# Two graph-attention layers on one core: every engine's order written by a list scheduler inside the kernel, fixed buffers, and two products moved

## The chip, the cores and the metric

The kernel runs as one program on 1 core of one Trainium2 chip. The metric is the device time of one execution in microseconds (us). The core's engines each run their own instruction stream in the order in which it was written: PE multiplies matrices, DVE and ACT do elementwise work, POOL does little here, and SP issues the transfers. An instruction waits on semaphores for what other engines must have done, and everything behind it on its engine waits too.

## The reference, cut to what matters

32 graphs with 512 nodes and 512 features each; `adj` is a 0/1 matrix with ones on its diagonal. A graph attention layer with 4 heads of 256 features is followed by one with a single head of 512.

```python
def gat_layer(x, mask, W, a_src, a_dst, bias, concat):
    xl = (x @ W).reshape(B, N, H, F)                                   # projection
    asrc = jnp.einsum('bnhf,hf->bnh', xl, a_src)
    adst = jnp.einsum('bnhf,hf->bnh', xl, a_dst)
    e = leaky_relu(asrc[:, :, None, :] + adst[:, None, :, :], 0.2)     # N x N per head
    e = jnp.where(mask[..., None], e, -1e9)
    attn = softmax(e, axis=1)
    out = jnp.einsum('bsdh,bshf->bdhf', attn, xl)                      # product
    return (out.reshape(B, N, H * F) if concat else out.mean(axis=2)) + bias

h = jnp.maximum(_layernorm(x), 0.0)
h = elu(gat_layer(h, mask, W1, att_src1, att_dst1, b1, concat=True))
h = gat_layer(h, mask, W2, att_src2, att_dst2, b2, concat=False)
return x + h
```

## The kernel before, in words

All of it is f32 on PE. For each graph PE does five things:

- four transposes of the normalized input (tiles `pht`, into `ht`);
- the first projection (tiles `pxl_*`, into `xl`): 28 groups of matmuls by a scheme of seven products of blocks instead of eight, whose block sums `hs` DVE forms (lines L336 to L339) and whose partial results ACT copies (L360, L362) or DVE adds (L365) from a PSUM bank into `xl`. A name such as `pxl_0b` is unit 0, bank b; a bank that was copied is written again by a later group, which must wait for the copy;
- the first product (`po`, L420): 4 heads, two groups of 4 matmuls each, weights of attention `p` times `xl`;
- the second projection (`pxm_*`, 14 groups, same scheme), into `xl2`;
- the second product (`po`, L484): 4 groups.

Only graph 0's first projection is done without the scheme (L388), while the weights' columns of scores are still being formed on DVE (L135); the sums of the weights (L109 to L112) come after it.

The softmax of one head (class `Soft`) is a chain over engines. `rows` sends the source scores through a small DRAM buffer and back, spread over all partitions (`das`, `oas`). `first` makes for each of four tiles a Prelu on ACT (L285), a masked minimum on DVE (L288, one custom instruction with the turned mask `mt`) and an Exp with a sum on ACT (L292); then Ln (L295), three small DVE operations and a transpose on DVE. `turn` sends that through DRAM again (`drr<-orr`, then `orr<-drr`, L249 and L255). `second` forms the weights `p`: per pair of tiles two DVE operations (L314), one DVE addition of the mask over both (L319), then two Exps on ACT (L321). The masks are turned by transposing transfers, four for a graph (L225), on SP's queue.

The order on PE is written out by hand in the loop over graphs: the first product of graph i+1, then the first projection of graph i+2, the second product of graph i, the second projection of graph i+1, and so on. What DVE, ACT and SP do comes from the framework's own scheduler, by the place in the program and a few priorities (`URGENT`); buffers rotate in pools. At the start PE does graph 0's first projection, graph 1's transposes, graph 0's first product and then graph 1's first projection. At the end stand graph 31's second projection, graph 30's second product, graph 31's second product.

Of the kernel before, what the change touches and what calls it, by code (L numbers as in the profile page):

```python
# [1 line left out]

# [19 lines left out]
URGENT = 300  # L22


def rows_of(ap, n):

    return bass.AP(tensor=ap.tensor, offset=ap.offset, ap=[[0, n], [1, ap.shape[-1]]])


@with_exitstack  # L30
def tile_gat(
# [30 lines left out]

    nc = tc.nc
# [8 lines left out]
    W = FH + 2  # L72
    assert N == 512 and D == 512 and DO == D and FH == 256 and H == 4

    const = ctx.enter_context(tc.tile_pool(name="const", bufs=1))
    work = ctx.enter_context(tc.tile_pool(name="work", bufs=2))
    psum = ctx.enter_context(tc.tile_pool(name="psum", bufs=1, space=PSUM))
    dram = ctx.enter_context(tc.tile_pool(name="dram", bufs=2, space=DRAM))

    nc.scalar.preload_act_table_set("natural_log_exp_and_others")  # L80


    identf = const.tile([P, P], F32, name="identf")
    make_identity(nc, identf)
    diag = const.tile([P, P], BF16, name="diag")
    nc.vector.tensor_scalar(diag, identf, -1.0, BIG, op0=OP.add, op1=OP.mult)
    half = const.tile([P, NT], F32, name="half")
# [5 lines left out]
    KQ = KT // 2  # L93
    w1_sb = const.tile([P, 7, KQ, H // 2, W], F32, name="w1_sb")
    KH = FT // 2
    W2H = DO // 2 + 1
    w2_sb = const.tile([P, 7, KH, W2H], F32, name="w2_sb")
    b1_sb = const.tile([P, FT], F32, name="b1_sb")
    b2_sb = const.tile([P, DO], F32, name="b2_sb")
    xl = const.tile([P, NT, H, W], F32, name="xl")  # L100
    xl2 = const.tile([P, NT, DO + 2], F32, name="xl2")

    def halves(w_sb):

        return {(0, 0): w_sb[:, 0], (0, 1): w_sb[:, 6], (1, 0): w_sb[:, 1], (1, 1): w_sb[:, 2]}

    def sums_of_weights(w_sb):
        b11, b21, b22, t4, t1, t2, t3 = (w_sb[:, i] for i in range(7))
        nc.vector.tensor_sub(t1, t3, b11)  # L109
        nc.vector.tensor_sub(t2, b22, t1)  # L110
        nc.vector.tensor_sub(t3, b22, t3)
        nc.vector.tensor_sub(t4, b21, t2)  # L112

    def weights1():
        at = halves(w1_sb)
        for c in range(2):
            for r in range(2):
                for k in range(KQ):
                    row = (r * KQ + k) * P
                    nc.sync.dma_start(  # L120
                        at[r, c][:, k, :, 2:],
                        w1[row : row + P, :].rearrange("p (j c f) -> p c j f", j=H // 2, c=2)[:, c],
                    )

    def scores1(j):

        at = halves(w1_sb)
        for c in range(2):
            for a, v in enumerate((as1, ad1)):
                bc = work.tile([P, FH], F32, tag="l", name=f"a1_{a}_{j}_{c}", bufs=3)  # L130
                nc.sync.dma_start(bc, rows_of(v[2 * j + c], P))
                for r in range(2):
                    for k in range(KQ):
                        junk = work.tile([P, FH], F32, tag="xr", name=f"j1_{a}_{j}_{c}_{r}_{k}", bufs=2)
                        nc.vector.scalar_tensor_tensor(  # L135
                            junk, at[r, c][:, k, j, 2:], 1.0, bc, op0=OP.mult, op1=OP.mult,
                            accum_out=at[r, c][:, k, j, a : a + 1],
                        )

    def weights2():  # L140

        at = halves(w2_sb)
        for (r, c), t in at.items():
            nc.sync.dma_start(
                t[:, :, 1 - c : W2H - c],
# [4 lines left out]
        nc.sync.dma_start(b1_sb, b1.rearrange("(c p) -> p c", p=P))  # L150
        nc.sync.dma_start(b2_sb, rows_of(b2, P))
        part = const.tile([P, 2, FT, 2], F32, name="part")
        for a, v in enumerate((as2, ad2)):
            bc = work.tile([P, DO], F32, tag="l", name=f"a2_{a}", bufs=3)
            nc.sync.dma_start(bc, rows_of(v[0], P))
            for (r, c), t in at.items():
                for k in range(KH):
                    junk = work.tile([P, DO], F32, tag="xr", name=f"j2_{a}_{r}_{c}_{k}", bufs=2)
                    nc.vector.scalar_tensor_tensor(
                        junk[:, : DO // 2], t[:, k, 1 - c : W2H - c], 1.0,  # L160
                        bc[:, c * DO // 2 : (c + 1) * DO // 2], op0=OP.mult, op1=OP.mult,
                        accum_out=part[:, a, r * KH + k, c : c + 1],
                    )
        for a in range(2):
            for r in range(2):
                g = part[:, a, r * KH : (r + 1) * KH, :]
                col = slice(0, 1) if a == 0 else slice(W2H - 1, W2H)
                nc.vector.tensor_add(at[r, a][:, :, col], g[:, :, 0:1], g[:, :, 1:2])
        sums_of_weights(w2_sb)

    XT, ADJ, HT, MASK, MASKT = {}, {}, {}, {}, {}

    def load(b):
        XT[b] = []
        for t in range(NT):
            xt = work.tile([P, D], F32, tag="x", name=f"x{b}_{t}", bufs=4)
            nc.sync.dma_start(xt, x[b, t * P : (t + 1) * P, :])
            XT[b].append(xt)

    def load_adj(b):  # L180
        ADJ[b] = []
        for t in range(NT):
            a = work.tile([P, N], I32, tag="adj", name=f"adj{b}_{t}", bufs=2)
            nc.sync.dma_start(a, adj[b, t * P : (t + 1) * P, :])
            ADJ[b].append(a)

    def norm(b):

        stats = work.tile([P, NT, nc.vector.BN_STATS_DIM], F32, tag="stats", name=f"stats{b}")
# [244 lines left out]
    def x2(b):  # L434

        if b < B - 1:
            return xl2
# [225 lines left out]
```

## Time and profile before

| | us |
|---|---|
| median of 3 runs (lowest, highest) | 3093.64 (3086.43, 3096.56) |
| the profiled execution | 3093.88 |
| span of its profile | 3092.1 |
| PE busy in it | 2967.6 (96%) |
| DVE busy | 2445.8 (79%) |
| ACT busy | 1785.8 (58%) |
| mean granted clock of PE | 0.99 |

The time of an execution is 1.8 us above its span. PE is busy for 96% of the span, so its time is the span less what it waits for; shares of DVE and ACT are averages over stages in which they are full and others in which they wait. A matmul's record runs past the start of the next one (they are pipelined), so distances from start to start are used where a rate is meant.

### The profile page before, as it was taken

The numbers are of one execution on the slowest core, as the hardware profiler recorded it, in microseconds if no ns is written. First come the engines' busy times: TensorE is split into PE (matmuls) and PEld (weight loads), VectorE is DVE, ScalarE is ACT, GpSimd is POOL, SyncE is SP. The second block draws the span as 40 slices with busy tenths as digits, with TensorE's granted clock in tenths as the row PEclk, the third lists the DMA queues.
The fourth block names the chain that finished last, engine by engine and source line by source line (L and its number), as shares of the span: only waits on it lengthen the run. The fifth ranks groups of instructions, "written<-read, shape, count | busy, mean of one in ns | idle before, by whom it ended". The sixth has DMA issues, their size and how long they took to land.

```text
span 3092.1 us, 33891 instructions
## 1 busy us (share of the span) xinstructions
PE 2967.6 (96%) x10768; PEld 2000.2 (65%) x10768; DVE 2445.8 (79%) x5534; ACT 1785.8 (58%) x3873; POOL 33.9 (1%) x38
## 2 busy tenths in 40 slices
PE   5799999999999999999999999999999999999997
PEld 4466676666766666766766766667666667666664
DVE  7688877788887788777788777888877888777874
ACT  3466665566665566565566555666655665655662
POOL 0000000000000000000000000000000000000000
PEclk8899999999999999999999999999999999999999
DMA  6022233232333232332222332323332323322212
GB/s 208 24 89 93 93 105 97 75 99 91 99 103 99 72 95 91 106 99 89 86 86 93 110 93 76 96 90 102 103 96 75 93 91 108 99 82 80 79 66 72
DMA packets 196020, 286.07 MB, mean 93 GB/s; under 512 B 92032, under 2 KB 97152, under 8 KB 195840
## 3 DMA queue, kind: packets, MB, share of 16 engines
q1 hardware_dynamic: 195840, 283.91, 29.6%
q8 instruction: 84, 1.38, 0.2%
q14 instruction: 96, 0.79, 0.1%
HBM read 232.53 MB, written 34.54 MB: 86 GB/s over the span
## 4 chain that ended last, share of the span: by engine, by line
PE 50%; DVE 27%; DMA 13%; SPq 5%; issue 3%; ACT 2%; POOL 0%; DVEq 0%; ACTq 0%; POOLq 0%
PE po L484 11%; DVE p L314 8%; DMA orr<-drr 6%; DVE p L319 6%; PE po L420 5%; SPq L225 4%; PE pxm_0a L353 4%; PE pxm_1a L353 4%; DVE l L288 3%; PE pxl_2a L353 3%; PE pxl_3a L353 3%; DMA oas<-das 3%; PE pxl_1a L353 3%; DVE h L429 2%; PE pxm_1b L353 2%
## 5 line engine op out<-in xcount | busy, mean ns | idle before, releaser
L420 PE MATMUL po<-p,xl 128*128 128x512 f32 x2048 | 891.4, 595 | 39.8 <-ACT p L321 39.8
L420 PEld LDWEIGHTS po<-p,xl 128*128 128x128 f32 x2048 | 390.0, 191 | 522.7 <-issue 449.9
L321 ACT ACTIVATE p<-p,lo 128x512 f32<-128x512 f32 x640 | 438.3, 713 | 390.3 <-DVE p L319 390.1
L314 DVE SCALAR_TENSOR_TENSOR p<-orr,lo 128x512 f32<-128x512 f32 x640 | 458.8, 742 | 140.0 <-DMA orr<-drr 131.8
L285 ACT ACTIVATE l<-oas,sc 128x512 f32<-128x512 f32 x640 | 431.0, 711 | 123.8 <-DMA oas<-das 115.3
L288 DVE CUSTOM_DVE_ANT_0 l<-l,mt 128x512 f32<-128x512 f32 x640 | 422.0, 681 | 60.9 <-ACT l L285 60.7
L292 ACT ACTIVATE l<-l,low 128x512 f32<-128x512 f32 x640 | 454.6, 711 | 16.6 <-DVE low L288 13.9
L484 PE MATMUL po<-xl,p 128*128 128x512 f32 x1024 | 451.8, 594 | 9.0 <-ACT p L321 9.0
L319 DVE TENSOR_TENSOR p<-p,m 128x1024 f32<-128x1024 f32 x320 | 387.7, 1212 | 0.1
L427 ACT ACTIVATE e<-po,b_sb 128x512 f32<-128x512 f32 x256 | 173.9, 680 | 301.2 <-PE po L420 293.9
L484 PEld LDWEIGHTS po<-xl,p 128*128 128x128 f32 x1024 | 192.3, 190 | 229.4 <-issue 209.6
L428 DVE TENSOR_SCALAR e<-e 128x512 f32<-128x512 f32 x256 | 107.0, 418 | 113.9 <-ACT e L427 113.7
L429 DVE SCALAR_TENSOR_TENSOR h<-po,b_sb,e 128x512 f32<-128x512 f32 x256 | 191.0, 746 | 5.4
L353 PE MATMUL pxm_1a<-w_sb,h 128*128 128x257 f32 x768 | 182.5, 379 | 0.0
L353 PE MATMUL pxm_0a<-w_sb,h 128*128 128x257 f32 x768 | 182.5, 379 | 0.0
L353 PEld LDWEIGHTS pxm_0a<-w_sb,h 128*128 128x128 f32 x768 | 145.2, 189 | 34.7 <-issue 9.1
L353 PEld LDWEIGHTS pxm_1a<-w_sb,h 128*128 128x128 f32 x768 | 145.4, 189 | 21.6
L353 PE MATMUL pxm_1b<-w_sb,hs 128*128 128x257 f32 x512 | 121.9, 380 | 1.9 <-DVE hs L336 1.9
L353 PE MATMUL pxm_0b<-w_sb,hs 128*128 128x257 f32 x512 | 121.7, 380 | 0.0
L292 ACT ACTIVATION_READ_ACCUMULATOR l<-l,low 128x1 f32 x640 | 120.6, 188 | 0.0
L353 PE MATMUL pxl_0b<-w_sb,hs 128*128 128x258 f32 x248 | 69.3, 403 | 44.5 <-ACT xl L360 44.5
L216 DVE TENSOR_SCALAR m<-adj 128x512 bf16<-128x512 int32 x128 | 51.6, 423 | 75.9 <-DMA adj<-in_adj_dram 75.9
(129 smaller groups left out, 3904.0 us busy)
## 6 DMA issues: line engine op xcount, KB each, us to landing
orr<-drr SPq DMA_DIRECT2D x160, 512.0 KB, 4.0
x<-in_x_dram SPq DMA_DIRECT2D x128, 256.0 KB, 3.3
adj<-in_adj_dram SPq DMA_DIRECT2D x128, 256.0 KB, 2.9
oas<-das SPq DMA_DIRECT2D x64, 512.0 KB, 3.7
xr<-in_x_dram SPq DMA_DIRECT2D x128, 256.0 KB, 4.6
out_dram<-xr SPq DMA_DIRECT2D x128, 256.0 KB, 2.0
oas<-das SPq DMA_DIRECT2D x32, 256.0 KB, 3.3
drr<-orr SPq DMA_DIRECT2D x160, 4.0 KB
```

The lines of the kernel that those rows point to most:

```text
L225: nc.sync.dma_start_transpose(MASKT[b][:, :, t * P : (t + 1) * P], MASK[b][:, t, :])
L285: nc.scalar.activation(e, self.asr[i][:, j, :], AF.Prelu, bias=ad[:, d : d + 1], alpha=SLOPE)
L288: nc.vector.tensor_tensor_reduce(out=e, in0=e, in1=MASKT[self.b][:, d, :], scale=-1.0, scalar=BIG, op0=OP.add, op1=OP.min, accum_out=low[: ...
L292: nc.scalar.activation(e, e, AF.Exp, bias=low[:, d : d + 1], scale=-1.0, accum_out=tot[:, d : d + 1])
L314: nc.vector.scalar_tensor_tensor(p[:, u, :], rr[:, 0, :], lo[:, 0, j, u : u + 1], rr[:, 1, :], op0=OP.add, op1=OP.max,)
L319: nc.vector.tensor_add(pp, pp, MASK[self.b][:, t : t + 2, :])
L321: nc.scalar.activation(p[:, u, :], p[:, u, :], AF.Exp, bias=lo[:, 1, j, u : u + 1])
L353: nc.tensor.matmul(ps, left[n][:, k, m * P : (m + 1) * P], right(w_sb[:, n - 1], k), start=(first and k == 0), stop=(k == kh - 1), skip_gr ...
L420: nc.tensor.matmul(ps, xl[:, s, h, 2 + f * P : 2 + (f + 1) * P], p[:, s, :], start=(s == 0), stop=(s == NT - 1),)
L427: nc.scalar.activation(e, ps, AF.Exp, bias=bias)
L429: nc.vector.scalar_tensor_tensor(H1[b][:, g, :], ps, bias, e, op0=OP.add, op1=OP.max)
L484: nc.tensor.matmul(ps, p[:, s, d * P : (d + 1) * P], v[:, s, 1 : DO + 1], start=(s == 0), stop=(s == NT - 1),)
```

## The change

A class `Program` records every instruction after the setup as a job: its engine, a cost in us written beside it by hand, the keys it reads and writes, and a function that emits it. `order` then runs a list schedule over all jobs: PE's jobs keep the order of the program; each other engine (ACT, DVE, POOL, SP) takes, of the jobs that are ready by the recorded costs, the one with the earliest latest start, counted back from the end. The instructions are emitted in that order with the framework's scheduler switched off for all engines. Pools are replaced by fixed tiles handed out in turn (`Slots`). Besides:

- graph 1's first projection stands ahead of graph 0's first product. For this graph 0's projected features go to places that are not yet in use (`xl0`: parts of `w2_sb`, `xl2` and `hs`), since `xl` takes graph 1's;
- at the end, of graph 29's second product one group stands ahead of graph 31's second projection and three behind it, followed by graph 30's second product (its features lie over `w1_sb`); before, graph 29's stood one graph earlier;
- the mask is added to `p` tile by tile (4 additions of 512 instead of 2 of 1024), and so is the bias `b2` to the residual;
- a graph's mask is turned by one transposing transfer of 128x2048 instead of four of 128x512;
- some small operations on DVE are merged. The matmuls are the same in number and shape.

```diff
+class Slots:
+    def take(self):
+        s = self.free.popleft()
+        return (self.name, s), self.tiles[s]
+    def give(self, key):
+        self.free.append(key[1])
+
+class Program:
+    CROSS, SAME = 0.15, 0.1
+    DMA_LEAD, DMA_TAIL, DMA_RATE = 1.2, 1.0, 230e3
+    def add(self, engine, cost, reads, writes, emit, size=None):
+        ...
+        self.jobs.append((engine, cost, deps - {n}, emit, size))
+    def order(self):
+        ...
+        for j in reversed(range(n)):
+            end = min((late[s] - self.latency(j, s) for s in after[j]), default=0.0)
+            if jobs[j][0] == "PE":
+                if pe is not None:
+                    end = min(end, late[pe])
+                pe = j
+            late[j] = end - jobs[j][1]
+        ...
+            if e == "PE":
+                j = tensor.popleft()
+            else:
+                while soon[e] and soon[e][0][0] <= t:
+                    k = heappop(soon[e])[1]
+                    heappush(ready[e], (late[k], k))
+                j = heappop(ready[e])[1]
+        ...
-        for t in range(NT):
-            nc.sync.dma_start_transpose(
-                MASKT[b][:, :, t * P : (t + 1) * P], MASK[b][:, t, :]
-            )
-            yield
+        prog.add(
+            "SP", 2.2, every, [tk],
+            lambda: nc.sync.dma_start_transpose(
+                mt.rearrange("p t d r -> p (t d) r"), m.rearrange("p t n -> p (t n)")
+            ),
+            300e3,
+        )
...
-                pp = p[:, t : t + 2, :]
-                nc.vector.tensor_add(pp, pp, MASK[self.b][:, t : t + 2, :])
+                dve(
+                    0.59, [key, mk + (u,)], [key], nc.vector.tensor_add,
+                    p[:, u, :], p[:, u, :], m[:, u, :],
+                )
...
+    run(project1_first(given))
+    ...
+    run(project1(1, left1))
+    weights2()
+    ...
+    first_product(0)
+    sums_of_weights(w2_sb, lambda ix: [("w2", ix), ("w2s", ix)], 1.15)
+    for i in range(B):
+        ...
+        if 1 <= i < B - 2 or i == B - 1:
+            g = min(i - 1, B - 3)
+            residual(g)
+            rest = gather2(g, S2.pop(g))
+            if i < B - 2:
+                run(rest)
+            else:
+                next(rest)
+        ...
+        if i == B - 1:
+            run(rest)
+            residual(i - 1)
+            run(gather2(i - 1, S2.pop(i - 1)))
+        S2[i].second(0)
+    residual(B - 1)
+    run(gather2(B - 1, S2.pop(B - 1)))
+    with tc.manual_schedule():
+        prog.emit()
```

In the changed kernel all rows have a helper's line, and tiles have the names of slots: `mm` are the six PSUM banks, `tp` the two banks of transposes, `p` the three buffers of weights of attention, `x` the input, `xr` the four shared buffers (for the exponentials that `e` held before, and the residual), `l` and `low` those of `first`, `z` the scores.

PE, the start, before: graph 1's transposes, graph 0's first product, graph 1's first projection.

```order
L206 MATMUL pht_3_630<-identf,x_3_242 128x128 x4
L420 MATMUL po_0_637<-p_1_0_442,xl 128x512 x4
L420 MATMUL po_1_657<-p_1_0_442,xl 128x512 x4
L420 MATMUL po_2_666<-p_1_1_583,xl 128x512 x4
L420 MATMUL po_3_686<-p_1_1_583,xl 128x512 x4
L420 MATMUL po_4_700<-p_1_2_646,xl 128x512 x4
L420 MATMUL po_5_715<-p_1_2_646,xl 128x512 x4
L420 MATMUL po_6_724<-p_1_3_675,xl 128x512 x4
L420 MATMUL po_7_733<-p_1_3_675,xl 128x512 x4
L353 MATMUL pxl_0a<-w_sb,ht_540 128x258 x2
```

And after, at the end of graph 1's first projection:

```order
L265 MATMUL mm_121<-w_sb,ht 128x258 x2
L265 MATMUL mm_126<-w_sb,ht 128x258 x2
L265 MATMUL mm_122<-p_97,w_sb 128x512 x4
L265 MATMUL mm_123<-p_97,w_sb 128x512 x4
L265 MATMUL mm_124<-p_98,xl_79 128x512 x4
L265 MATMUL mm_125<-p_98,xl_79 128x512 x4
```

The 28 groups of graph 1's first projection moved from behind graph 0's first product to ahead of it.

ACT, a graph in the middle, before, from the last exponentials of a first product (`e`, L427) to the first copies of the next first projection. The rows with `p_2_0` are the Exps that finish the weights for the second product, those with `l_2_0` and `tot_2_0` its sums and Ln:

```order
L321 ACTIVATE p_1_3_8209<-p_1_3_8209,lo_1_1_7916 128x512 x2
L292 ACTIVATE l_2_0_1_8235,tot_2_0_8230<-l_2_0_1_8235,low_2_0_8229 128x512
L292 ACTIVATE l_2_0_2_8239,tot_2_0_8230<-l_2_0_2_8239,low_2_0_8229 128x512
L292 ACTIVATE l_2_0_3_8243,tot_2_0_8230<-l_2_0_3_8243,low_2_0_8229 128x512
L427 ACTIVATE e_4_8276<-po_4_8271,b_sb 128x512
L295 ACTIVATE tot_2_0_8230<-tot_2_0_8230 128x4
L427 ACTIVATE e_5_8291<-po_5_8286,b_sb 128x512
L427 ACTIVATE e_6_8300<-po_6_8295,b_sb 128x512
L427 ACTIVATE e_7_8309<-po_7_8304,b_sb 128x512
L360 ACTIVATE xl<-pxl_0a 128x258
L321 ACTIVATE p_2_0_8364<-p_2_0_8364,lo_2_0_8182 128x512
L360 ACTIVATE xl<-pxl_0b 128x258
```

And after, in the same place (`xr` with `b_sb` are the exponentials 3 to 7, `low_120` alone is the Ln, `p_96` the weights for the second product):

```order
L254 ACTIVATE xr_92<-mm_123,b_sb 128x512
L254 ACTIVATE l_93,low_120<-l_93,low_120 128x512
L254 ACTIVATE l_94,low_120<-l_94,low_120 128x512
L254 ACTIVATE low_120<-low_120 128x4
L254 ACTIVATE xr_89<-mm_124,b_sb 128x512
L254 ACTIVATE xr_90<-mm_125,b_sb 128x512
L254 ACTIVATE xr_91<-mm_121,b_sb 128x512
L254 ACTIVATE xr_92<-mm_122,b_sb 128x512
L254 ACTIVATE xl<-mm_126 128x258
L254 ACTIVATE p_96<-p_96,z_114 128x512
L254 ACTIVATE xl<-mm_123 128x258
```

The Ln moved from behind the exponential 4 to ahead of it; the first Exp of the second product's weights still stands between the first two copies of the projection.

PE, the end, before: the last group of graph 31's second projection, then the second products of graphs 30 and 31.

```order
L353 MATMUL pxm_1a<-w_sb,h_18680 128x257 x4
L484 MATMUL po_0_18903<-xl_81,p_2_0_18792 128x512 x4
L484 MATMUL po_1_18949<-xl_81,p_2_0_18792 128x512 x4
L484 MATMUL po_2_18956<-xl_81,p_2_0_18792 128x512 x4
L484 MATMUL po_3_18963<-xl_81,p_2_0_18792 128x512 x4
L484 MATMUL po_0_18978<-xl,p_2_0_18938 128x512 x4
```

And after:

```order
L265 MATMUL mm_123<-w_sb,h_81 128x257 x4
L265 MATMUL mm_125<-xl_79,p_97 128x512 x4
L265 MATMUL mm_124<-xl_79,p_97 128x512 x4
L265 MATMUL mm_122<-xl_79,p_97 128x512 x4
L265 MATMUL mm_121<-w_sb,p_98 128x512 x4
L265 MATMUL mm_126<-w_sb,p_98 128x512 x4
L265 MATMUL mm_123<-w_sb,p_98 128x512 x4
L265 MATMUL mm_125<-w_sb,p_98 128x512 x4
L265 MATMUL mm_124<-xl,p_96 128x512 x4
```

Three groups of graph 29's second product now stand between graph 31's second projection and graph 30's second product.

More of the change, by code (lines that the diff above doesn't have):

```diff
@@ L72, in tile_gat @@
     W = FH + 2
[L73 to L84, printed above, removed]
```

935 lines of the change are left out of this document (565 added, 370 removed).

## The prediction

> **What bounds the kernel now.** I read the page first, then who waited for whom on PE, then the stages in windows, then the order of time at the three places where PE waits. The page (busy us, share, count; granted clock in tenths by slices):
>
> ```profile
> PE 2967.6 (96%) x10768; PEld 2000.2 (65%) x10768; DVE 2445.8 (79%) x5534; ACT 1785.8 (58%) x3873; POOL 33.9 (1%) x38
> PEclk8899999999999999999999999999999999999999
> ```
>
> PE is the bound, so what can be gained is what PE waits, and what it runs slowly. Its waits (total, times, longest):
>
> ```profile
> PE pxl_0b L353 <- ACT xl L360: 44.5, 28, 2.7
> PE po L420 <- ACT p L321: 39.8, 9, 15.4
> PE pht L206 <- DVE x L201: 9.6, 1, 9.6
> PE po L484 <- ACT p L321: 9.0, 1, 9.0
> PE pht L206 <- ACT ht L208: 6.9, 1, 6.9
> PE pxl_2g L353 <- DVE xl L365: 4.3, 4, 1.4
> PE pxl L388 <- DVE j L135: 3.3, 2, 2.9
> PE pxm_1b L353 <- DVE hs L336: 1.9, 1, 1.9
> PE pxm_0a L353 <- DVE hs L338: 1.5, 1, 1.5
> ```
>
> The windows cut the span at PE's first transpose, at the ends of the first products of graphs 0 and 1, and at the last second projection (length, busy of PE, PEld, DVE, ACT, POOL, clock, share of the transfers, GB/s):
>
> ```profile
> 9.61:127.09 117.48, 71.01 (x224) 44.76 (x225) 91.39 (x282) 48.20 (x99) 2.94 (x2) 0.83 0.41 126
> 127.09:209.56 82.47, 78.89 (x306) 55.85 (x305) 62.86 (x150) 53.45 (x117) 1.01 (x1) 1.00 0.18 60
> 209.56:3021.60 2812.04, 2763.23 (x10065) 1866.05 (x10064) 2256.34 (x5041) 1668.23 (x3626) 28.21 (x28) 1.00 0.30 92
> 3021.60:3092.10 70.50, 54.48 (x177) 33.56 (x175) 30.87 (x52) 14.69 (x30) 0.00 (x0) 0.93 0.21 70
> ```
>
> PE idles 46.5 us in the first, 3.6 in the second, 48.8 in the third, 16.0 in the last. The third is 30 graphs, all alike:
>
> ```profile
> 234.06 7.04 PE L484 MATMUL po<-xl,p 128*128 128x512 f32 x16
> 2864.35 7.04 PE L484 MATMUL po<-xl,p 128*128 128x512 f32 x16
> 2956.04 13.91 PE L484 MATMUL po<-xl,p 128*128 128x512 f32 x32
> ```
>
> Between the first two lie 28 graphs, (2864.35 - 234.06) / 28 = 93.94 us each; the last pair is one graph without a wait, 91.69. So the steady stage loses 2.25 us a graph, 63.0 in all: the waits, and a slow matmul behind each.
>
> **The change, term 1: the start.** In the first window DVE is busy 91.39 of 117.48 us and PE waits for the first softmaxes, with graph 1's projection, which needs none of them, queued behind. The change puts that projection first. Its matmuls are the same; its copies and additions (16 on ACT, 12 on DVE) come earlier into DVE's full stretch, but they were due before graph 1's softmax anyway. With the projection moved, what ends last is DVE's work for both softmaxes. In before it starts with the first masked minimum and ends with the last mask addition of graph 1:
>
> ```profile
> 46.07 0.69 DVE L288 CUSTOM_DVE_ANT_0 l<-l,mt 128x512 f32<-128x512 f32 x1 [2.88 <-ACT l L285]
> 202.27 1.22 DVE L319 TENSOR_TENSOR p<-p,m 128x1024 f32<-128x1024 f32 x1
> 46.07:204.30 158.23, 124.48 (x321) 0.87 0.19 63
> 46.07:121.00 74.93, 64.68 (x182) 0.73 0.23 73
> ```
>
> 124.5 us of work took 158; in its dense first half, up to graph 0's last weights, DVE idled 10.25. In after the same work is one dense stretch, since the projection no longer splits it. The stretch starts somewhat earlier: the rows of `att_src1` and `att_dst1` are issued ahead of half of `w1` and of `adj`, but the whole mask must now be ready before its one transposing transfer, and the scores' return from DRAM stands behind that transfer on SP. I take 42, between 46.07 as before and 39. Add 124.5, 3 for idle (between 0 and 10.25) and 5 from the last weights to the end of the product (before: 209.56 - 203.5 = 6.1). That gives 174.5 instead of 209.56: a gain of **35**. Best case 39 + 124.5 + 5 = 168.5, 41 gained; worst 46.07 + 124.5 + 10.25 + 6.1 = 186.9, 23 gained. `weights2` moves too, but its DVE work (L159, L109 to L112) lies in both stretches; graph 0's second projection is behind it and waits some us for these sums, inside the 174.5, where DVE is what counts.
>
> A slow clock belongs to this term. After long waits the products ran slowly, after short ones not:
>
> ```profile
> 70.14 9.97 PE L420 MATMUL po<-p,xl 128*128 128x512 f32 x16 [13.17 <-ACT p L321]
> 107.14 1.98 PE L420 MATMUL po<-p,xl 128*128 128x512 f32 x4 [2.40 <-ACT p L321]
> ```
>
> Sixteen matmuls take 7.04 in the steady stage, 9.97 here: 2.9 lost. The Trainium skill (TensorE: Matmul & The Clock Gate, "Part 1: The HAM clock gate") says that about 3.4 us of idleness halve the clock until PE has been busy as long again; the two rows agree. By it, gaps of over 3.4 us before each of eight heads would cost 8 x 2.9 = 23 us and the gain would be 12, not 35. By the trace alone I expect gaps of about 1.5: a head is 4 masked minima, 4 operations of L314 and 4 additions, about 8.4 us of DVE by the means of 681, 742 and 678 ns (the last from an addition of 512, below), against 6.9 on PE.
>
> **Term 2: the steady stage.** The wait of 44.5 us, in a graph in the middle (PE, ACT, DVE, SP):
>
> ```profile
> 1341.22 1.14 PE L353 MATMUL pxl_0b<-w_sb,hs 128*128 128x258 f32 x4 [1.55 <-ACT xl L360]
> 1340.17 0.72 ACT L321 ACTIVATE p<-p,lo 128x512 f32<-128x512 f32 x1 [4.43 <-DVE p L319]
> 1340.80 0.37 ACT L360 ACTIVATE xl<-pxl_0b 128x258 f32<-128x258 f32 x1
> 1336.93 2.07 DVE L314 SCALAR_TENSOR_TENSOR p<-orr,lo 128x512 f32<-128x512 f32 x3 [3.94 <-DMA orr<-drr]
> 1338.92 1.22 DVE L319 TENSOR_TENSOR p<-p,m 128x1024 f32<-128x1024 f32 x1
> 1325.15 5.99 SPq L225 DMA_TRANSPOSE mt<-m  x4
> 1331.18 0.55 SPq L249 DMA_DIRECT2D drr<-orr  x1
> 1332.87 0.34 SPq L255 DMA_DIRECT2D orr<-drr  x1
> ```
>
> PE waits for a copy out of the bank; the copy stands on ACT behind the first Exp of the second product's weights; this waits for DVE, DVE for the return from DRAM, and that trip was issued behind four mask transposes of 5.99 us. The changed order still has that Exp between the first two copies, and the transpose still ahead of the trip. But two things bring the Exp forward. The mask is added by tiles, so the Exp waits for two operations of L314 and one short addition instead of three and a long one: about 1.4 + 0.7 instead of 3.2 us, 1.1 earlier. And the Ln that starts the trip stands ahead of exponential 4 on ACT instead of behind it: one group of the first product, 3.4 us, earlier. Together 4.5, where the longest wait is 2.7. So the wait goes, if the transpose holds SP no longer than before. Its single transfer shows in no row: the bound below is one of the four, about 1.3, above it four, 5.99; I take the upper end, since the same bytes are moved. The additions cost DVE
>
> ```profile
> L319 DVE TENSOR_TENSOR p<-p,m 128x1024 f32<-128x1024 f32 x320 | 387.7, 1212 | 0.1
> L338 DVE TENSOR_TENSOR hs<-hs,ht 128x512 f32<-128x512 f32 x31 | 21.1, 682 | 0.0
> ```
>
> 2 x 682 - 1212 = 152 ns a pair, 320 pairs, 49 us over the run; in the steady stage DVE idles 556 of 2812, which hides it; were DVE full there, it would come whole. The 4 waits for DVE's additions (4.3 us) I let go with the rest. Of 63.0 I take a gain of **57**, leaving 0.2 us a graph for places I did not see; bounds 0 and 63.
>
> **Term 3: the end.**
>
> ```profile
> 3049.84 13.92 PE L484 MATMUL po<-xl,p 128*128 128x512 f32 x32
> 3072.77 15.70 PE L484 MATMUL po<-xl,p 128*128 128x512 f32 x32 [9.01 <-ACT p L321]
> ```
>
> The last softmax takes 3072.77 - 3049.84 = 22.9 us from the end of graph 31's second projection, with 13.9 of product to cover it. Three more groups of 3.44 make 24.2: the wait of 9.0 goes, and the 1.8 that the last product ran slowly; the one group put ahead of the projection covers the 1.9 and 1.5 for its sums. 14.2 in all; graph 30's Exps now share ACT and DVE with this, so I take **12**, between 5 and 14. What follows the last matmul is unchanged.
>
> **Sum.** 35 + 57 + 12 = 104; 3093.88 - 104 = **2990**. It is made against the profiled execution, 0.2 above the median of the runs.
>
> **Rivals.**
> - *The steady wait stays.* For it: the Exp still stands ahead of the copy, and nothing orders DVE by when transfers really land; the costs are fixed numbers in the code. Against: the 4.5 us above. Only terms 1 and 3: 3093.88 - 47 = 3047. With half the wait, 3018.
> - *The start gains little:* the queue of SP holds the scores' return behind the mask's transfer, and DVE starts late and idles; or heads come with long gaps and a slow clock. For it: 10.25 us of idling in the dense stretch. Against: after the wait of 2.40 us the product was hardly slower. With 2.9 us lost at each of eight heads 23 go, and 12 instead of 35 are gained: 3013.
> - *The order does not do what it says, no change:* waits move to other places as large, since a fixed order can't follow late events. For it only that PE's steady work (91.69) is untouched. 3094.
> - *Slower:* the one transfer of 16 blocks holds SP much longer than four of 4. Every graph's trip to DRAM stands behind it. Above 5.99 + (4.5 - 1.5) = 9 us PE waits for all the rest, 30 graphs; terms 1 and 3 are used up at 47 / 30 = 1.6 us beyond the old loss of 2.1, so from about 9 + 3.7 = 12.7 us on the kernel is slower. At 15 us: 3094 + 30 x 2.3 = 3163. Against: four transposes move the same bytes in 5.99.
>
> **How the numbers follow.** Forecast 0.68, from 2976 (41, 63 and 14 gained) to about 3012 (23, 52 and 7); the steady wait in whole or half 0.17 (3018 to 3047), the start alone 0.08 (3013), no change 0.03, slower 0.04. The range 2968 to 3047 holds the first three; its lower end is a little under the best sum, since DVE's work need not all stand before the last weights. A difference of 0.3%, 9 us, is about what a measurement of this kernel can tell: faster 0.93, same 0.03, slower 0.04.
>
> **What would show it.** Right: PE busy for about 99% of the span; in the list of waits no copy of `xl` with over 10 us in all; the end of graph 1's first product near 174; DVE at over 90% from 42 to there; the last second product without a wait; steady graphs 91.7 to 92.0 apart. Wrong: PE waiting at the third or seventh group of each first projection for ACT (term 2); gaps of several us before each head of graphs 0 and 1, with a clock under 1 (term 1); a mask transpose of over 9 us on SP.

## The result, and the profile after

The changed kernel takes **2981.82 us** (median of 4, 2980.66 to 2982.33) against 3092.87 (3086.43 to 3096.56): a ratio of 0.9643, 95% interval 0.9626 to 0.9659. The forecast was 2990. The profiled execution took 2982.33, with a span of 2980.6, 111.5 less than before.

From the page, PE's line (busy us, share, count) and the granted clock by slices:

```profile
PE 2948.7 (99%) x10768; PEld 1994.8 (67%) x10768; DVE 2472.1 (83%) x5772; ACT 1800.4 (60%) x3873; POOL 43.5 (1%) x38
PEclk9999999999999999999999999999999999999999
```

PE was busy 96% and is busy 99%. Of its waits the two with the largest totals are these (total, times, longest), and the copies of `xl`, 44.5 us before, hold it for 0.4:

```profile
PE mm L265 <- ACT p L254: 12.4, 13, 2.8
PE tp L265 <- DVE x L257: 10.0, 1, 10.0
...
PE mm L265 <- ACT xl L254: 0.4, 1, 0.4
```

The windows show the dense start and the 30 graphs behind it (length, busy of PE, PEld, DVE, ACT, POOL, clock, share of the transfers, GB/s):

```profile
42.00:171.76 129.76, 115.12 (x391) 69.60 (x390) 125.51 (x331) 91.03 (x192) 1.01 (x1) 0.99 0.34 104
174.50:2900.00 2725.50, 2725.45 (x10005) 1853.66 (x10003) 2267.85 (x5226) 1676.34 (x3613) 39.69 (x29) 1.00 0.31 94
```

In these 2725.5 us PE idles for less than 0.1. Now the order of time, at the places that the prediction named: the first masked minimum, the last mask additions of graph 1, the product after them and the projection behind it; second products 27 graphs apart; and the end.

```profile
42.55 0.69 DVE L257 CUSTOM_DVE_ANT_1 l<-l,mt 128x512 f32<-128x512 f32 x1 [0.45 <-ACT l L254]
165.00 1.29 DVE L257 TENSOR_TENSOR p<-p,m 128x512 f32<-128x512 f32 x2
164.56 7.36 PE L265 MATMUL mm<-p,xl 128*128 128x512 f32 x16 [1.39 <-ACT p L254]
171.76 1.03 PE L265 MATMUL mm<-w_sb,ht 128*128 128x258 f32 x4
287.80 13.91 PE L265 MATMUL mm<-xl,p 128*128 128x512 f32 x32
2763.16 13.91 PE L265 MATMUL mm<-xl,p 128*128 128x512 f32 x32
2961.82 1.99 PE L265 MATMUL mm<-xl,p 128*128 128x512 f32 x4 [1.06 <-ACT p L254]
2964.35 12.30 PE L265 MATMUL mm<-xl,p 128*128 128x512 f32 x28 [0.54 <-ACT p L254]
```

Graph 1's first product ends at 171.76 (209.56 before), steady graphs are (2763.16 - 287.80) / 27 = 91.68 apart (93.94 before), and the last product, which waited 9.0, waits 1.06 and 0.54. The same place in a middle graph that the prediction showed of before (PE, ACT, DVE, SP):

```profile
1271.92 1.03 PE L265 MATMUL mm<-w_sb,ht 128*128 128x258 f32 x4
1260.85 0.20 ACT L254 ACTIVATE low<-low 128x4 f32<-128x4 f32 x1
1272.99 0.39 ACT L254 ACTIVATE xl<-mm 128x258 f32<-128x258 f32 x1 [0.18 <-PE mm L265]
1273.27 0.71 ACT L254 ACTIVATE p<-p,z 128x512 f32<-128x512 f32 x1
1258.98 0.69 DVE L257 CUSTOM_DVE_ANT_1 l<-l,mt 128x512 f32<-128x512 f32 x1
1263.02 0.44 DVE L257 STREAM_TRANSPOSE rr<-low 128x256 f32<-128x256 f32 x1
1270.54 1.41 DVE L257 SCALAR_TENSOR_TENSOR p<-rr,z 128x512 f32<-128x512 f32 x2
1259.70 1.96 SPq L392 DMA_TRANSPOSE mt<-m  x1
1263.49 0.54 SPq L260 DMA_DIRECT2D drr<-rr  x1
```

Counted from the projection's first matmul, the Exp of `p` came 5.88 us after it before (1340.17 - 1334.29) and comes 1.35 after it now. And SP is held 1.96 us by the one transposing transfer, not 5.99: the trip `drr<-rr` no longer stands behind it. The 5.99 of that graph is above the usual: in 11 of 14 middle graphs of before the four transfers hold SP 5.14 to 5.16 us.

Something else has moved here. The transposing transfer begins as soon as the softmax's last masked minimum has ended, and this row of before (its projection begins at 1334.29) and the one above show that it ends 9.2 us ahead of the projection before (1324.43 + 0.68) and 12.25 now (1258.98 + 0.69):

```profile
1324.43 0.68 DVE L288 CUSTOM_DVE_ANT_0 l<-l,mt 128x512 f32<-128x512 f32 x1
```

### The profile page after: what moved, and what is told of

It reads as the page before. It is cut to its first block, busy times and chain, and to the rows that moved or that the text cites. A ratio compares the mean times of both kernels' runs of the same rounds, so it can differ in the third digit from the quotient of the medians.

```text
span 2980.6 us, 34136 instructions
## 1 busy us (share of the span) xinstructions
PE 2948.7 (99%) x10768; PEld 1994.8 (67%) x10768; DVE 2472.1 (83%) x5772; ACT 1800.4 (60%) x3873; POOL 43.5 (1%) x38
## 4 chain that ended last, share of the span: by engine, by line
PE 96%; DVE 3%; ACT 0%; DMA 0%; issue 0%; SPq 0%; POOL 0%
PE mm L265 94%; PE tp L265 2%; DVE p L257 2%; DVE xr L257 1%; DVE l L257 0%; DVE h L257 0%; ACT p L254 0%; DMA x<-in_x_dram 0%; ACT l L254 0%; DMA rr<-drr 0%; DVE stats L257 0%; ACT xr L254 0%; DVE w_sb L257 0%; DVE xl L257 0%; DVE m L257 0%
## 5 line engine op out<-in xcount | busy, mean ns | idle before, releaser
L265 PE MATMUL mm<-p,xl 128*128 128x512 f32 x2016 | 873.2, 593 | 7.4 <-ACT p L254 7.3
L265 PE MATMUL mm<-w_sb,hs 128*128 128x257 f32 (+1 forms) x3024 | 719.2, 380 | 2.1 <-DVE hs L257 1.7
L265 PEld LDWEIGHTS mm<-w_sb,hs 128*128 128x128 f32 x3024 | 570.5, 190 | 85.8 <-DVE hs L257 2.1
L254 ACT ACTIVATE p<-p,z 128x512 f32<-128x512 f32 x640 | 441.1, 714 | 160.4 <-DVE p L257 159.9
L265 PE MATMUL mm<-w_sb,ht 128*128 128x258 f32 x2112 | 511.6, 381 | 0.2
L265 PE MATMUL mm<-w_sb,h 128*128 128x257 f32 x2048 | 471.5, 380 | 1.4 <-DVE h L257 1.1
L257 DVE SCALAR_TENSOR_TENSOR p<-rr,z 128x512 f32<-128x512 f32 x640 | 457.3, 744 | 1.2 <-DMA rr<-drr 1.2
L254 ACT ACTIVATE l<-as,z 128x512 f32<-128x512 f32 x640 | 438.0, 709 | 7.2 <-DMA as<-das 5.3
L265 PE MATMUL mm<-xl,p 128*128 128x512 f32 x992 | 431.8, 592 | 1.6 <-ACT p L254 1.6
L257 DVE TENSOR_TENSOR p<-p,m 128x512 f32<-128x512 f32 x640 | 424.1, 685 | 0.0
```

What stands on the lines that cost most here:

```text
L254: prog.add("ACT", cost, reads, writes, lambda: nc.scalar.activation(*a, **k))
L257: prog.add("DVE", cost, reads, writes, lambda: f(*a, **k))
L265: f(*a, **k)
```

## The experiments

Each was timed beside the kernel before. That kernel took 3080 to 3083 on the chips of the experiments (medians), 10 to 13 us less than on the first; the changed kernel, timed again on one of them, took the same as on the first.

**The changed kernel again** (no edit).

> The changed kernel itself, unaltered, beside the kernel before on the chip of these experiments, since the kernel before ran about 10 us faster there (3083) than on the first chip. Theory (a fixed order with room for late transfers gives the same time on each chip): 2980 to 2983. Rival (this chip is faster for any kernel): 2970 to 2975.

Measured: 2982.15 (2981.78 to 2984.41), before 3079.84, as the theory said. All runs of the kernel before lie between 3076 and 3097, all of the changed one between 2980.7 and 2984.4. So the experiments on the changed kernel are compared with 2982.15, and only the one on the kernel before with its own neighbour.

### The start

**The projection back behind the first product.**

```
-    run(project1(1, left1))
     weights2()
...
-        if i >= 1 and i + 1 < B:
+        if i + 1 < B:
             run(project1(i + 1, left1))
```

> The changed kernel with one thing put back: graph 1's first projection stands behind graph 0's first product again, as before; orders on the other engines are planned anew for it. Theory (the place of the projection made the gain at the start): graph 1's softmax can't begin until its projection has run, so DVE has no second half of dense work while graph 0's product runs; the end of graph 1's first product goes from 171.8 back toward 209.6, to about 202 (between 195 and 210), and the time from 2982 to about 3012 (3005 to 3020). Rival (the dense order on DVE and ACT made it, the projection's place little): the end of that product stays under 180 and the time under 2990.

Measured: 2996.19 (2996.14 to 2996.35), 14 us slower. In order of time, PE's first head, the last group of graph 0's first product, and the projection behind graph 1's:

```profile
66.50 9.76 PE L265 MATMUL mm<-p,w_sb 128*128 128x512 f32 x16 [13.23 <-ACT p L254]
99.58 3.70 PE L265 MATMUL mm<-p,hs 128*128 128x512 f32 x8 [0.84 <-DVE h L257]
184.68 1.03 PE L265 MATMUL mm<-w_sb,ht 128*128 128x258 f32 x4
```

and the window up to the end of graph 0's first product:

```profile
42.00:103.10 61.10, 36.03 (x86) 15.64 (x84) 56.70 (x173) 36.87 (x76) 1.01 (x1) 0.80 0.43 138
```

beside that of the kernel before, from its first masked minimum to the same end:

```profile
46.07:127.09 81.02, 37.87 (x86) 16.90 (x85) 65.88 (x184) 40.41 (x82) 1.01 (x1) 0.75 0.21 68
```

This lies between theory and rival: graph 1's product ends 12.9 us later, not 30. Of the 37.8 us gained at the start, 24.9 (209.56 to 184.68) come without the projection's new place. Graph 0's first product ends at 103.3 (99.58 + 3.70) in the old PE order, where it ended at 127.09 before. DVE idles 4.4 of 61 us there; in before it idled 15 of 81, and had 9 us more to do by then. What follows, from there to the end of graph 1's product, takes 81.6 us (103.10 to 184.68) and took 82.5: this part stays as long as the projection stands in its old place. The projection was not moved by itself in the kernel before, so what it is worth there is open.

**More work on DVE in the start.**

```
-                for k in range(KH):
+                for k in list(range(KH)) * 2:
                     jk, junk = xrs.take()
```

> The changed kernel with the 32 products for the second layer's score columns (128x256, 435 ns and 98 ns for the sum's readout) run twice on DVE in the dense start, 17 us of work more between 42 and 110 us, with the same result; PE's order is unchanged. Theory (at the start DVE is the bound, 125.5 us busy of 129.8): the end of graph 1's first product goes from 171.8 to about 186 (183 to 190) and the time to about 2996 (2992 to 2999). Rival (PE's own order sets that time, DVE has room for it): under 2987.

Measured: 2997.48 (2995.86 to 2997.74), 15.3 us slower; the end of graph 1's first product at 186.05. In the listing of groups from 20 to 130 us (busy us, mean ns) the products are

```profile
L257 DVE SCALAR_TENSOR_TENSOR xr<-w_sb,l 128x256 f32<-128x256 f32 x64 | 23.3, 416 | 0.0
```

against 11.6 for 32 in the changed kernel: 11.7 more, and 1.9 for the readouts of their sums (5.0 for 3.1), 13.6 in all and not the 17 expected. The product ends 14.3 later. So, as the theory said, DVE's work in the start costs time about one for one.

### The steady stage

**Four transposing transfers for one**, all orders unchanged.

```
-            lambda: nc.sync.dma_start_transpose(
-                mt.rearrange("p t d r -> p (t d) r"), m.rearrange("p t n -> p (t n)")
-            ),
+        def turn():
+            for t in range(NT):
+                nc.sync.dma_start_transpose(mt[:, t], m[:, t, :])
```

> The changed kernel with the mask turned by four transfers of 128x512 instead of one of 128x2048; every engine's order is the same, word for word, and the planner still reckons with its old cost. SP is then held about 6.0 us instead of 1.96, and the second product's trip to DRAM is issued about 2.2 us later. Theory (the Ln ahead of an exponential and the mask added by tiles gave more room than the wait needed): that is taken up by the 1.3 us that the arrived row waits for DVE and by the 3 us between the copy and PE's need of the bank; steady graphs stay 91.7 us apart, the start may lose up to 4 us since the scores' return stands behind the transfer: 2982 to 2987. Rival (the short transfer is what took the steady wait away): PE waits for a copy of xl again, about 1.5 us a graph: about 3027 (3015 to 3045).

Measured: 2984.55 (2983.14 to 2987.16), 2.4 slower. SP and ACT in a middle graph whose projection begins at 1276.62:

```profile
1264.41 6.01 SPq L392 DMA_TRANSPOSE mt<-m  x4
1270.53 0.55 SPq L260 DMA_DIRECT2D drr<-rr  x1
1278.39 0.72 ACT L254 ACTIVATE p<-p,z 128x512 f32<-128x512 f32 x1 [0.31 <-DVE p L257]
```

Counted from the projection, the trip is issued 2.3 us later than in the changed kernel, the Exp comes at 1.77 instead of 1.35, and PE waits for no copy beyond the 0.4 of the start. So the four transfers are bearable in this order, as the theory said, but not by its reason of the early Ln: the row that the trip sends was ready at 1268.17 and waited 2.4 us for SP, and the trip goes out right behind the transfers. It is early since these begin 12.2 us ahead of the projection (1276.62 - 1264.41), where they began 9.1 ahead in before (1334.29 - 1325.15).

**Eight transfers**, of 128x256 (the loop above, twice as fine).

> As the run with four transfers, with eight of 128x256: SP is held about 11 to 12 us, the trip is issued about 7.7 us later than in the changed kernel, and the first Exp of the second product's weights comes about 6.4 us later with the copy behind it in ACT's order. Theory (a late Exp ahead of a copy is what stops PE, and beyond about 9 us on SP it does): PE waits about 2.9 us in each of some 30 graphs for ACT's copy of xl, steady graphs about 94.6 apart, and the start loses up to 9: about 3072 (3050 to 3095). Rival (this Exp does not hold up PE, whatever SP does): steady graphs stay under 92.2 apart and the time under 3000.

Measured: 3034.64 (3032.21 to 3036.32), 52 slower. The wait is back, in the list of waits and at one place (SP, ACT, PE; the projection begins at 1295.00, and all lines of the kernel stand one or two lower here):

```profile
PE mm L266 <- ACT xl L255: 30.3, 30, 2.2
```

```profile
1280.28 11.91 SPq L394 DMA_TRANSPOSE mt<-m  x8
1300.70 0.72 ACT L255 ACTIVATE p<-p,z 128x512 f32<-128x512 f32 x1 [4.25 <-DVE p L258]
1301.75 2.01 PE L266 MATMUL mm<-w_sb,hs 128*128 128x258 f32 x8 [1.37 <-ACT xl L255]
```

The mechanism is the theory's; its size was half of what was expected, 1.37 us at this place for 2.9, since the first of the eight transfers starts 14.7 us before the projection here and the single one 12.2 in the changed kernel, so the trip was delayed by 5.7, not 7.7. Of the 52 us, 6.3 are lost in the start, where graph 1's first product ends at 178.08.

**The kernel before, with one transposing transfer.**

```
-            nc.sync.dma_start_transpose(
-                MASKT[b][:, :, t * P : (t + 1) * P], MASK[b][:, t, :]
-            )
+            if t == NT - 1:
+                nc.sync.dma_start_transpose(
+                    MASKT[b].rearrange("p t d r -> p (t d) r"),
+                    MASK[b].rearrange("p t n -> p (t n)"),
+                )
...
-                    out=e, in0=e, in1=MASKT[self.b][:, d, :], scale=-1.0, scalar=BIG,
+                    out=e3, in0=e3, in1=MASKT[self.b][:, :, d, :], scale=-1.0, scalar=BIG,
```

> The kernel before with one thing of the change: the mask is turned by one transfer of 128x2048 instead of four of 128x512. The order on ACT and SP in the steady stage is that of before otherwise, with the Ln behind exponential 4, the mask added in pairs, and the first Exp between the first two copies. Theory (the row's trip stood 2.76 us behind four transfers, and the single one holds SP 1.96 us): the trip and with it the Exp come 2.7 us earlier, which is as much as the longest steady wait; PE's wait for ACT's copy of xl falls from 44.5 us to under 5, steady graphs go from 93.9 to about 92 apart, and the time falls by about 50 (35 to 63). Rival (it was the Ln's place and the long mask addition, as the prediction had it, that made the Exp late): the wait stays over 30 us and the time falls by under 15.

Measured: 3034.94 (3033.53 to 3036.03) against 3083.01, a ratio of 0.9844 (0.9824 to 0.9863): 48 us from one transfer. SP and ACT, with the projection's start at 1312.91, and two second products 27 graphs apart:

```profile
1303.79 1.72 SPq L226 DMA_TRANSPOSE mt<-m  x1
1307.14 0.54 SPq L251 DMA_DIRECT2D drr<-orr  x1
1315.93 0.72 ACT L324 ACTIVATE p<-p,lo 128x512 f32<-128x512 f32 x1 [1.56 <-DVE p L322]
326.38 7.04 PE L487 MATMUL po<-xl,p 128*128 128x512 f32 x16
2805.05 7.04 PE L487 MATMUL po<-xl,p 128*128 128x512 f32 x16
```

The Exp comes at 3.0 instead of 5.9, the 44.5 us of waiting for copies are gone from the list, and graphs are 91.80 apart, as the theory said; the prediction's two reasons weren't needed for it. (The 93.94 of before is from the first chip, where that kernel took 10 us more than here, so 91.80 and 93.94 don't add up to the 48.)

**The mask in pairs again**, and **pairs, four transfers and the late Ln**, which puts back all that was thought to make the Exp late.

```
-                    p[:, u, :], p[:, u, :], m[:, u, :],
+                    pp, pp, m[:, u - 1 : u + 1, :],
```

> The changed kernel with the mask added to two tiles at once, as before, everywhere; the planner, which reckons with 1.13 us for a pair, puts the Ln of the second layer behind exponential 4 by itself, as before, and the first Exp of the second product's weights behind the third copy instead of the first. Theory (a steady graph has room for the Exp as soon as it doesn't stand ahead of a copy that is due): no steady wait, DVE busy about 49 us less, the dense start about 2.4 us shorter: 2978 (2974 to 2984). Rival (the mask added tile by tile and the early Ln are needed): PE waits for copies of xl, 1 us a graph or more: over 3005.

> The run with the mask in pairs, and four transposing transfers on top of it, and the Ln of the second layer held behind exponential 4: everything that made the Exp late in the kernel before is back, and only the planned order is left, which has the Exp behind the third copy. Every engine's order is that of the run with pairs. Theory (where the Exp stands among the copies decides, not when it comes): the Exp comes about 5.9 us after the projection's start as in before, the fourth copy behind it at 7.0, and PE needs that bank's sum at about 8.7: no steady wait, and the time is that of the run with pairs plus 0 to 5 for the start: 2982 (2977 to 2988). Rival (the Exp has to be early): PE waits as in before, 1.5 us in each of 30 graphs: over 3020.

Measured: 2986.80 (2986.47 to 2987.21) and 2988.11 (2987.25 to 2990.43). In both, steady graphs are 91.68 apart. In the second the Exp comes as late as in the graph shown of before, 5.83 us after the projection's start at 1275.18, but behind three copies, the third of which is the first row here:

```profile
1278.86 0.39 ACT L254 ACTIVATE xl<-mm 128x258 f32<-128x258 f32 x1 [1.35 <-DVE p L257]
1281.01 0.72 ACT L254 ACTIVATE p<-p,z 128x512 f32<-128x512 f32 x1 [1.76 <-DVE p L257]
```

So the place among the copies also suffices. The first expectation missed by 9: the pairs were to shorten the start by 2.4 and cost 1.9 there (graph 1's first product ends at 173.63) and 2.8 at the end, where the last product waits 2.30 and then runs slowly. A head's first Exp is later with pairs, which may be why; that was not tested apart.

**Another rule of priority.**

```
-                    heappush(ready[e], (late[k], k))
+                    heappush(ready[e], (k, k))
```

> The changed kernel with another rule for who goes first on ACT, DVE, SP and POOL: of the steps that are ready in the plan, the one that stands first in the program, not the one with the earliest due time; PE's order, the buffers and the costs are unchanged. Theory (due times from PE's order are what gives the copies and additions of the banks, the trips and the first head their place): PE waits for copies in each projection and the start is no longer dense, together 20 to 100 us: about 3030 (3000 to 3080). Rival (fixed buffers, PE's new order and the new cut of the work make the gain, and any sensible order of ready steps does): under 2992.

Measured: 3046.54 (3045.40 to 3047.77), 64 slower, as the theory said:

```profile
PE mm L265 <- ACT xl L254: 18.3, 32, 3.7
PE mm L265 <- DVE xl L257: 17.5, 31, 8.6
PE mm L265 <- ACT w_sb L254: 12.9, 1, 12.9
```

Copies and additions of the banks come late again: graph 1's first product ends at 183.91, 12.2 later, graphs are 92.89 apart, and one wait of 12.9 stands before the end (`w_sb` there is graph 30's second projection, which lies in the first weights' place).

### The end

**Graph 29's second product in one piece.**

```
-        if 1 <= i < B - 2 or i == B - 1:
-            g = min(i - 1, B - 3)
+        if 1 <= i < B - 1:
+            g = i - 1
             residual(g)
-            rest = gather2(g, S2.pop(g))
...
+            run(gather2(g, S2.pop(g)))
```

> The changed kernel with graph 29's second product put back whole into its place before graph 30's second projection, so that nothing is left over for the last graph: no group ahead of the last projection and no three groups behind it. Theory (those four groups cover the last softmax and the last sums): the last second product waits 9.0 us as it did before, the last projection 3.4 us, less what the planned order brings the softmax forward, so the time goes from 2982 to about 2993 (2989 to 2997). Rival (the planned order of ACT and DVE makes the last softmax short enough by itself): under 2986.

Measured: 2991.00 (2990.56 to 2991.75), 8.9 slower, as the theory said, with the wait before the last product back:

```profile
2968.81 16.31 PE L265 MATMUL mm<-xl,p 128*128 128x512 f32 x32 [10.53 <-ACT p L254]
```

The theory's other wait did not come back: the last second projection, with no group ahead of it, runs from 2920.01 to 2944.37 without a wait for its sums. So the planned order, and not the group ahead, is enough to take away the 1.9 and 1.5 us that before lost there.

### Two versions meant to be faster

**The sums of weight blocks on POOL** (`nc.gpsimd.tensor_sub` for `nc.vector.tensor_sub`, the columns of scores apart).

> A version meant to be faster: the eight sums of blocks of the two weight matrices (1.23 us each on DVE) go to POOL, all but the score columns, which stay on DVE as sixteen small steps less eight (8 of about 0.12 us); nothing else in the program is changed and the planner is given 2.5 us for each on POOL. DVE has about 8.8 us less to do before 110 us. Theory (DVE is the bound at the start and POOL is free): the end of graph 1's first product comes 5 to 9 us earlier and the time is about 2975 (2972 to 2978). Rival (POOL is much slower than planned, or slows DVE while it runs, so that graph 1's projection or the second projection waits for the sums): 2982 to 3000.

Measured: 2994.00 (2993.22 to 2994.88), 11.9 slower, which is the rival's outcome, by the second of its conditions: POOL slows DVE. POOL's own steps took 2.4 to 2.9 us, for the 2.5 planned. In order of time, the first three of them and two products on DVE, one ahead of them and one beside them:

```profile
14.75 7.54 POOL L291 TENSOR_TENSOR w_sb<-w_sb 128x1024 f32<-128x1024 f32 x3 [5.70 <-DMA w_sb<-in_L_gnn_W_dram]
14.33 0.42 DVE L257 SCALAR_TENSOR_TENSOR xr<-w_sb,p 128x256 f32<-128x256 f32 x1
15.02 2.59 DVE L257 SCALAR_TENSOR_TENSOR xr<-w_sb,p 128x256 f32<-128x256 f32 x1
```

A DVE step of 0.42 us lasts as long as the POOL step beside it, three times in a row (2.59, 2.55 and 2.56). The Trainium skill (SBUF — State Buffer, "Who interferes with whom") says that a DVE instruction with two inputs in SBUF contends with a GpSimd instruction that reads SBUF, over a pair of ports that the two engines share and that only one of them holds at a time; these rows agree. By the times on PE most of the loss stands early: graph 1's transposes begin at 50.55, 7.5 us after those of the changed kernel (43.07), and its first product ends at 182.54, 10.8 later.

**The end of the activation on ACT, for graphs 0 and 1.**

```
+                if b < 2:
+                    act(0.62, [bk, "b1"], hk, h1[:, g, :], ps, AF.Relu, bias=bias)
+                    act(0.62, [ek], [ek], e, e, AF.Relu, bias=1.0, scale=-1.0)
+                    dve(0.59, [ek] + hk, hk, nc.vector.tensor_sub, h1[:, g, :], h1[:, g, :], e)
```

> A version meant to be faster: for the two first graphs alone, the end of the first layer's activation is taken from DVE, which bounds the start, to ACT, which there idles 38 of 124 us: ACT forms the positive part of sum and bias from the bank and one minus the exponential, cut at zero, and DVE only subtracts the two (0.69 us in place of 0.75 and 0.43). The result is the same. DVE has 0.49 us less for each of 16 groups, 13 of which fall into the dense start: 6.4 us; ACT has 1.36 us more for each, 18 in the start. Theory (a microsecond of DVE work in the start costs about 0.9 of time, as the run with the products twice showed): 2977 (2974 to 2980). Rival (ACT's two longer steps delay the Exps of the weights or the bank, and PE waits for ACT instead): 2982 to 2992.

Measured: **2978.34** (2978.13 to 2978.85), a ratio of 0.9660 (0.9647 to 0.9674) to before and 3.8 us under the changed kernel, all of whose runs, on two other chips, are slower. That is as the theory said, with graph 1's first product ending at 167.69. The stretch from 42 to 171.76, to set beside the one above (DVE 125.51, ACT 91.03):

```profile
42.00:171.76 129.76, 118.08 (x406) 73.92 (x406) 124.84 (x334) 109.83 (x232) 2.02 (x2) 0.97 0.37 106
```

ACT took up 19 us, and DVE used the time for what comes next.

## Why the prediction was right, and where it was not

**The sum.** 111.5 us were gained where 104 were forecast: 37.8 at the start (35), 63 in the steady stage (57), and the 10.7 that remain at the end (12). The time is 8 us under the forecast.

**Term 1.** Its numbers held: the first masked minimum at 42.55 (42), the last addition at 166.3 (169.5 by the sum), DVE busy 125.51 of 129.76, 97%, the product's end at 171.76 (174.5). Its reason held by a third. "The change puts that projection first" is worth 13 to 14 us by the run that puts it back; the other 25 come from the rest of the change, with the old PE order. The step that failed is "one dense stretch, since the projection no longer splits it", which gave the projection's place the whole of the idle time that goes. In the old PE order with the rest of the change, DVE starts 4.1 us earlier, idles 10.7 less and does 9.2 less work up to the end of graph 0's first product, and 0.9 are gained behind it; the sum is the 24.9. That 35 came out so near is in part chance: the size of the stretch was right, the reason for its being dense was not. That DVE's work bounds the changed start is shown by the products done twice and by the activation on ACT.

**The slow clock.** The waits before heads were short, 2.80 us at most, and little was lost, as the trace of before had let expect; the largest loss is the 2.2 us behind that wait of 2.80. Gaps over 3.4 us, which the rule that the prediction cites (the Trainium skill, TensorE: Matmul & The Clock Gate, "Part 1: The HAM clock gate") would have charged, did not occur. (The prediction takes 678 ns for an addition of 512; the row it shows for it says 682, and the 8.4 us stay.)

**Term 2.** "So the wait goes" was right, and more fully than the 57: nothing is left of 63. The mis-sized step is the transfer: "I take the upper end, since the same bytes are moved". It takes 1.96 us, near the lower bound of 1.3. With that, the trip in the middle graph was issued 5.3 us earlier against the projection, 2.75 of them because nothing stands ahead of it on SP and 2.6 because the row that it sends is ready earlier. For this last part the prediction's reason fails: that the Ln stood behind exponential 4, "one group of the first product, 3.4 us". Exponential 4 did not wait for PE in before, and the Ln began 1.3 us after the last masked minimum ended; now it begins 1.2 after it. What came earlier, by 3.1 us, is that masked minimum, and with it the transfer and the Ln. The rule of due times is not what brings it forward: in the run with the other rule of priority it ends 13.55 us ahead of the projection. What does was not tested. Of the 5.3 the Exp came 4.5 earlier: 1.3 are lost since DVE takes the arrived row later, and the additions by tiles gave back 0.5, not 1.1. That 4.5 was also the prediction's figure is chance. The runs show three things that each suffice: the short transfer in the old order; the planned order's earlier start of the transfer, with the additions by tiles and the four old transfers; and the Exp's place behind three copies, though it comes late.

**The additions.** 152 ns a pair were to cost 49 us of DVE, hidden. The groups give 424.1 us for 640 single ones against 387.7 for 320 pairs, 36.4 more. They are hidden in the steady stage, as said.

**Term 3.** 12 was forecast; the remainder is 10.7, and the run with the product in one piece loses 8.9. The wait of 9.0 went but for 1.06 + 0.54. The step "the one group put ahead of the projection covers the 1.9 and 1.5 for its sums" was not needed, by the same run.

**The rivals.** "The steady wait stays" did not happen, and the run with eight transfers shows at what price it would have: 1.37 us at 11.9 us on SP. "Slower" had the right place and mechanism: taken back by its 1.37 us, the wait would begin at 10.5 us on SP, or at 8.0 for a transfer that starts 2.5 us later, where the single one does (estimates from that run's rows; the prediction said 9). But the transfer got shorter instead. "The start gains little" fell with DVE's 97%.

## What to carry to other kernels

Where a bank's copy stands behind a step that waits for a trip through DRAM, look at the queue that issues the trip before the engines are re-planned: here one transfer instead of four gave 48 of about 100 us on the chips of the experiments, in the old order; in the planned order it is worth 2.4 by the medians, hardly more than the runs of one kernel differ. An expected gain that fits by its size is not yet explained: undo the parts one by one, since several of them may each be enough. In a start that is bound by one engine, price each step by what it takes there, and try the engine that idles and shares nothing with it.

## What the runs showed of the hardware that was not expected

SP is held by the number of transposing transfers more than by their bytes. With the same mask each time, it is held 1.72 to 2.04 us by one of 128x2048 in the middle graphs of the changed kernel, 5.14 in most graphs by four of 128x512 (1.29 each; 6.01 in the graph shown) and 11.40 in most by eight of 128x256 (1.43 each; 11.91 in the graph shown).

The clock can fall after less than the 3.4 us of idleness that the Trainium skill states (TensorE: Matmul & The Clock Gate, "Part 1: The HAM clock gate"). In the changed kernel's start a wait of 2.80 us was enough, in order of time and by the window over it (clock 0.68):

```profile
99.38 5.75 PE L265 MATMUL mm<-p,hs 128*128 128x512 f32 x8 [2.80 <-ACT p L254]
```

```profile
99.38:103.00 3.62, 3.52 (x6) 1.15 (x6) 3.62 (x12) 1.79 (x3) 0.00 (x0) 0.68 0.01 2
```

Eight such matmuls take about 3.5 in the steady stage (half of 7.04). The length of the wait does not decide it alone. In the run with the mask in pairs a wait of 2.30 us before the last product was followed by a clock of 0.66 (from 2965.54 to 2969.20), and one of 2.94 us, longer than either, by four matmuls at full speed (1.98, as after 2.40 us in before) and a clock of 1.00 (from 166.25 to 168.40):

```profile
2965.54 15.77 PE L265 MATMUL mm<-xl,p 128*128 128x512 f32 x32 [2.30 <-ACT p L254]
166.25 1.98 PE L265 MATMUL mm<-p,xl 128*128 128x512 f32 x4 [2.94 <-ACT p L254]
```

Here the measurement differs from the rule's figure; what else decides, these runs do not show.

The kernel before varied by 20 us over chips and runs, the changed one by 4. What made the difference was not looked into.
